# Two convolutions in 32x32 products: blocks of two adjacent rows, or of the two halves of one image

## The chip, the cores and the metric

The kernel runs on one core of a Trainium2 chip. The time is the device time of one execution in microseconds; the median of several runs is compared. The five engines that appear below are TensorE (PE, with its weight loads as PEld), VectorE (DVE), ScalarE (ACT), GpSimd (POOL) and SyncE (SP, which here only issues transfers).

## The reference

Four layers of the form x = x + conv(groupnorm(x)) act on a tensor of 16 images, 16 channels and 256 x 256 pixels in float32. Only the first two layers matter here:

```python
x = x + _L0_conv_ref(_gn(x), L0_conv_weight)      # 3x3 convolution, circular in y and x (written with FFTs)
x = x + _L1_conv_ref(_gn(x), L1_conv_filter_w)    # 5x5 kernel filter_w[..., :, None] * eye(5), zero padding of 2
```

The group norm has 8 groups of 2 channels, over a whole image. The second kernel is diagonal: it takes the pixel (y + d, x + d) for d from -2 to 2, so it has five taps, each with a 16 x 16 matrix over channels. Layers 2 and 3 (a pole-residue layer and a quantised 3x3 convolution) follow; they read the result of layer 1 from DRAM.

## The kernel before

Layers 0 and 1 form one stage, with an instruction order that is written out by hand. Each image b is held in SBUF as `xs[b % 2]`, its layer-1 input as `vs[b % 2]`. The 128 partitions are four quads of 32 (`quads`), and each quad holds 16 channels times two adjacent rows of the image, the parity of the row being the upper or lower 16 lanes (`lanes(p, i)`). The four quads of x are four bands of rows.

A matmul works on one quad of the input and one quad of the output, so it is a 32x32 product, and sixteen such tiles of the array can work at once. With two adjacent rows in the block, 16 input lanes and 16 output lanes of different parity stand for different offsets in y. For layer 0, the outputs of the lower lanes are also shifted by one column, so that 2 row steps times 4 column steps, eight products of 512 columns (two row pairs), cover the 3x3 taps (`products0`, L449). For layer 1 three products of 257 columns (one row pair) cover the five diagonal taps (`products1`, L471). The residual is added by putting ones into the scaled weights (`scaled`).

`load` (L269 to L274) brings an image in four parts, each as DMAs of 16 partitions and 8 or 9 rows, 1 KB per row, on SP's queue. `edges` (L374, L375) copies the circular columns on POOL, `see` (L378) takes statistics on DVE. The `Chain` class makes the group norm: aggregate, a product with the `group` table on PE (L311), another (L322), a reciprocal root on DVE, and a constant per lane (L340); POOL scales the weights (L389).

`leave0` (L455, L456) takes a bank out of PSUM on ACT into `vs` and DVE takes its statistics. `halo` (L433) copies the rows that neighbouring bands need, on POOL for one side and on ACT for the other. `pads` (L417 to L422) fills the padding with the mean on POOL. `leave1` (L479 to L489) takes layer 1's bank out on ACT, mends the outer column on DVE, takes statistics and stores x2d in DMAs of 16 partitions, half of them issued from POOL and half from SP. PSUM has seven banks for these products (`ps_v`) and one for the group norm.

The order of all this comes from `at(time, function, ...)`: every step gets a time in columns of a product, and the steps are issued on their engines sorted by it. `WEAVE` is the period of one image; layer 1 of image b is woven into layer 0 of image b + 1:

```python
    WEAVE = 4 * 8 * 2 * N + 8 * 3 * (N + 1)          # 22,552 columns
...
        t0 = b * WEAVE + (0, 4096, 9734, 16143)[u] + 1024 * p                                        # unit0
...
        t0 = (b + 1) * WEAVE + (8192, 8963, 13830, 14601, 15372, 20239, 21010, 21781)[s] + 1024 * q  # unit1
```

The index p (or q) is the quad that is contracted, the row group of the array. In these times each row group always has one unit in work, and the four are 1,024 columns apart. Within a step the four products go to the four output quads.

Of the kernel before, what the change touches and what calls it, by code (L numbers as in the profile page):

```python
# [71 lines left out]
def constants():  # L72
# [10 lines left out]
    def sin(a, b):  # L83
# [38 lines left out]
        "group": (p % 16 // 2 == q % 16 // 2) / 16.0,  # L122
        "first": p == 2 * c8,
# [13 lines left out]
        "res": np.concatenate([1.0 * (p % 32 == np.arange(32)[None, :] + 16),  # L137
                               1.0 * (p % 32 + 16 == np.arange(32)[None, :])], 1),
# [29 lines left out]
def layers(ctx, tc, x, w0, w1, w3, sw, bias, ty, tx, p1a, p1b, p1c, p2a, p2b, p2c, resa, resb,  # L168
# [61 lines left out]
    PW = N + 3  # L230
    VW = N + 5
    XS = N // 8 + 1
    WEAVE = 4 * 8 * 2 * N + 8 * 3 * (N + 1)

    def by_rows(d, p, i, lo, n):

        return d.rearrange("c (k t) w -> c t k w", t=2)[:, i, 32 * p + lo : 32 * p + lo + n, :]

    def lanes(p, i):
        return slice(32 * p + 16 * i, 32 * p + 16 * i + 16)  # L240

    quads = [slice(32 * r, 32 * r + 32) for r in range(4)]

    with ExitStack() as es:
# [10 lines left out]

        xs = [wp.tile([P, XS, PW], F32, tag=f"x{k}", name=f"x{k}") for k in range(2)]
        vs = [wp.tile([P, 4, 10, VW], F32, tag=f"v{k}", name=f"v{k}") for k in range(2)]

        def load(b, part):

            lo, n = 8 * part, 8 if part < 3 else 9
            for p in (0, 2, 1, 3):
                for i in range(2):
                    to, rows_ = xs[b % 2][lanes(p, i)], x[b]
                    k0, n_, at = lo, n, lo
                    if i == 0:
                        k0 -= 1
                        if p == 0 and part == 0:
                            nc.sync.dma_start(to[:, 0, 1 : 1 + N], rows_[:, N - 1, :])  # L269
                            k0, n_, at = 0, n - 1, 1  # L270
                    elif p == 3 and part == 3:
                        nc.sync.dma_start(to[:, XS - 1, 1 : 1 + N], rows_[:, 0, :])
                        n_ = n - 1
                    nc.sync.dma_start(to[:, at : at + n_, 1 : 1 + N], by_rows(rows_, p, 1 - i, k0, n_))  # L274

        for part in range(4):
            load(0, part)
        group, first, ones = table(wp, "group"), table(wp, "first"), table(wp, "ones")
        even, odd = table(wp, "real"), table(wp, "imag")
        res, eye = table(wp, "res"), table(wp, "eye")  # L280
        wt0 = wp.tile([P, 8, 32], F32, tag="wt0", name="wt0")
        nc.sync.dma_start(wt0.rearrange("p n m -> p (n m)"), w0)
        wt1 = wp.tile([P, 3, 32], F32, tag="wt1", name="wt1")
# [6 lines left out]
        for k, (w, n) in enumerate(((wt0, 8), (wt1, 3))):  # L290
            red = cell(32, "red")
            V.tensor_reduce(red, w.rearrange("p n m -> p m n"), AX.X, ADD)
            whole = wp.tile([P, 4, 32], F32, tag=f"sum{k}", name=f"sum{k}")
            V.tensor_scalar(whole, bc(red, 1, 4), -0.25, None, MUL)
            sums.append(whole.rearrange("p q m -> p (q m)"))
# [75 lines left out]
        def edges(b, part):  # L371
            lo, n = 8 * part, 8 if part < 3 else 9
            s = xs[b % 2][:, lo : lo + n]
            Q.tensor_copy(s[:, :, 0:1], s[:, :, N : N + 1])  # L374
            Q.tensor_copy(s[:, :, 1 + N : 3 + N], s[:, :, 1:3])  # L375

        def see(b, k):
            V.bn_stats(stats_of(st0s, b, "st0")[:, k, :], xs[b % 2][:, 2 * k : 2 * k + 2, 1 : 1 + N])  # L378
# [7 lines left out]
        def scaled(b, kind):  # L386
            n, wt, eyes = ((8, wt0, ((1, 0), (6, 1))), (3, wt1, ((1, None),)))[kind]
            w = sp.tile([P, n, 32], F32, tag=f"w{kind}s", name=f"w{kind}s")
            Q.tensor_scalar(w, wt, chains[b, kind].rs[:, 0:1], None, MUL)  # L389
            for k, e in eyes:  # L390
                tt(Q, w[:, k], w[:, k], eye if e is None else res[:, 32 * e : 32 * e + 32], ADD)
            (w0s, w1s)[kind][b] = w
# [17 lines left out]
        def pads(b):  # L410

            v, mu = vs[b % 2], chains[b, 1].g3[:, 0:1, 0]
            flat = v.rearrange("p g n w -> p (g n) w")
            me, mo = cell(1, "me"), cell(1, "mo")
            tt(Q, me, mu, even, MUL)
            tt(Q, mo, mu, odd, MUL)
            Q.tensor_copy(v[quads[0], 0, 0, :], mu[quads[0]].to_broadcast([32, VW]))  # L417
            Q.tensor_copy(v[quads[3], 3, 9, :], mu[quads[3]].to_broadcast([32, VW]))
            for lo in (0, VW - 2):
                Q.tensor_copy(flat[:, :, lo : lo + 2], bc(bc(mu[:, 0], 1, 40), 2, 2))  # L420
            Q.tensor_scalar(flat[:, :, 2:3], flat[:, :, 2 + N : 3 + N], odd, me, MUL, ADD)
            Q.tensor_scalar(flat[:, :, 2 + N : 3 + N], flat[:, :, 2 + N : 3 + N], even, mo, MUL, ADD)  # L422

        def halo(b, q, side):

            v, eng = vs[b % 2], (Q.tensor_copy if side else nc.scalar.copy)
            frm = (q + (1 if side else -1)) % 4
            g_to, g_from = slice(0, 4), slice(0, 4)
            if side and q == 3:
                g_to, g_from = slice(0, 3), slice(1, 4)  # L430
            if not side and q == 0:
                g_to, g_from = slice(1, 4), slice(0, 3)
            eng(v[quads[q], g_to, 9 if side else 0, 3 : 3 + N], v[quads[frm], g_from, 1 if side else 8, 3 : 3 + N])  # L433

        def unit0(b, u, p):

            t0 = b * WEAVE + (0, 4096, 9734, 16143)[u] + 1024 * p
            for n in range(8):
                at(t0 + 512 * n, products0, b, u, p, n)
            at(t0 + 4095.5, leave0, b, u, p)  # L440

        def products0(b, u, p, n):
            if n == 0:
                open_[p] = ps_v.tile([P, 512], F32, tag="ps_v", name="ps_0")
            ps = open_[p]
            e, t = divmod(n, 4)
            for q in range(4):
                lo = 8 * q + 2 * u + e
                nc.tensor.matmul(ps[quads[q]].rearrange("p (k w) -> p k w", k=2), lhsT=w0s[b][quads[p], n, :],  # L449
                                 rhs=xs[b % 2][quads[p], lo : lo + 2, t : t + N], start=n == 0, stop=n == 7)  # L450

        def leave0(b, u, p):
            ps = open_[p]
            to = vs[b % 2][:, p, 1 + 2 * u : 3 + 2 * u, 3 : 3 + N]
            nc.scalar.activation(to, ps.rearrange("p (k w) -> p k w", k=2), AF.Identity, bias=c0s[b])  # L455
            V.bn_stats(stats_of(st1s, b, "st1")[:, 4 * p + u, :], to)  # L456

        def unit1(b, s, q):

            t0 = (b + 1) * WEAVE + (8192, 8963, 13830, 14601, 15372, 20239, 21010, 21781)[s] + 1024 * q  # L460
            for n in range(3):
                at(t0 + 257 * n, products1, b, s, q, n)
            at(t0 + 770.5, leave1, b, s, q)

        def products1(b, s, q, n):
            if n == 0:
                open_[q] = ps_v.tile([P, 512], F32, tag="ps_v", name="ps_1")
            ps = open_[q]
            for p in range(4):
                lo = 2 * n  # L470
                nc.tensor.matmul(ps[quads[p], 0 : N + 1], lhsT=w1s[b][quads[q], n, :],  # L471
                                 rhs=vs[b % 2][quads[q], p, s + n, lo : lo + N + 1], start=n == 0, stop=n == 2)

        def leave1(b, s, q):
            ps, h = open_[q], s // 4
            if s % 4 == 0:
                outs[q] = op.tile([P, 4, N + 1], F32, tag="x2s", name="x2s")
            o = outs[q]
            nc.scalar.activation(o[:, s % 4, :], ps[:, 0 : N + 1], AF.Identity, bias=c1s[b])  # L479
            if s % 4 < 3:  # L480
                return
            e = cell(4, "fix")
            V.tensor_scalar(e, o[:, :, 0], odd, None, MUL)
            V.scalar_tensor_tensor(o[:, :, N], o[:, :, N], even, e, MUL, ADD)
            for k in range(2):
                V.bn_stats(stats_of(st2s, b, "st2")[:, 4 * q + 2 * h + k, :], o[:, 2 * k : 2 * k + 2, 1 : 1 + N])
            for i in range(2):
                for p in (0, 2, 1, 3):
                    (nc.sync if i else Q).dma_start(by_rows(x2d[b], p, i, 8 * q + 4 * h, 4),  # L489
                                                    o[lanes(p, i), :, 1 - i : 1 - i + N])  # L490

        for b in range(B):
            t = b * WEAVE
            for p in range(4):
                for u in range(4):
                    unit0(b, u, p)
                for s in range(8):
                    unit1(b, s, p)
            for q in range(4):
                at(t + 7800 + 700 * q, halo, b, q, 1)  # L500
                at(t + 23400 + 250 * q, halo, b, q, 0)
            for k in range(4):
                if b:
                    at(t - WEAVE + 900 + k if b > 1 else -30000 + k, load, b, k)
                at(t - WEAVE + 6500 + 3300 * k, edges, b, k)
                for n in range(4):
                    at(t - WEAVE + 6500 + 3300 * k + 300 * n, see, b, 4 * k + n)
# [926 lines left out]
```

## Time and profile before

| what | value |
|---|---|
| median of three runs | 4160.77 us (4160.36 to 4162.11) |
| the profiled execution | 4147.03 us |
| its span, first to last instruction | 4145.2 us |
| granted TensorE clock, mean | 0.943 |
| PE, PEld, DVE, ACT, POOL busy | 85, 67, 67, 53, 46% of the span |
| one slice of the page (a fortieth) | 103.6 us |

The page gives busy time for each engine and for groups of instructions: line, engine, operation, tiles, shape, count, then busy microseconds and mean nanoseconds of one, then the idle time before them and what ended it. In the view of one line's instructions, three durations are the smallest, median and largest in nanoseconds, and the two times after them are the first and last start. In the timeline, merged instructions stand with start, length and count. In the windows, each engine has its busy time and count, in the order PE, PEld, DVE, ACT, POOL (only PE and PEld where one line is asked for), then the granted clock, the DMA share and GB/s. A record that overlaps a window is counted as busy in it.

### The profile page before, as it was taken

What the parts mean: (1) busy time and instruction counts of PE and PEld (TensorE: products, weight loads), DVE (VectorE), ACT (ScalarE), POOL (GpSimd) and SP (SyncE); (2) the same over time, 40 slices, a digit from 0 to 9 for tenths busy, and PEclk for the clock granted to TensorE, in tenths of its full rate; (3) what the DMA queues carried; (4) which work ended last, traced back from release to release, by engine and by line L of the source; (5) the groups of instructions that cost most, each with busy time, mean ns of one, the idle gap of its engine ahead of it and who ended that gap; (6) DMA issues with size and microseconds to landing.
All of it is one profiled execution on the core that took longest, in us unless ns stands there. A gap on an engine that the chain in (4) does not pass through costs nothing. (4 is left out here: it accounts for less than half of the span.)

```text
span 4145.2 us, 175747 instructions
## 1 busy us (share of the span) xinstructions
PE 3539.6 (85%) x77336; PEld 2766.3 (67%) x77336; DVE 2759.2 (67%) x5153; ACT 2189.7 (53%) x3985; POOL 1906.9 (46%) x2878
## 2 busy tenths in 40 slices
PE   4899988989968999999966777776999999996777
PEld 3555555555537999999955555555888888883444
DVE  3555555555548888887765656654677777668998
ACT  1344444444425444444466666665454544448998
POOL 0334343433333434443276666663666766662222
PEclk9899999999959999999999999998999999997898
DMA  7666576756343545455356666667888888868998
GB/s 91 104 128 135 120 137 117 133 120 130 84 116 128 189 152 168 150 185 174 130 164 189 186 184 186 187 185 196 224 232 237 237 231 246 248 185 313 337 353 304
DMA packets 510974, 758.03 MB, mean 183 GB/s; under 512 B 53697, under 2 KB 419137, under 8 KB 501953
## 3 DMA queue, kind: packets, MB, share of 16 engines
q1 hardware_dynamic: 467200, 612.26, 54.2%
q0 software_dynamic: 43008, 134.52, 10.6%
q8 instruction: 608, 9.96, 1.0%
q14 instruction: 158, 1.29, 0.1%
HBM read 410.52 MB, written 336.07 MB: 180 GB/s over the span
## 5 line engine op out<-in xcount | busy, mean ns | idle before, releaser
L449 PE MATMUL ps<-x,w0s 32*32 32x512 f32 x16384 | 936.5, 643 | 36.1 <-issue 35.9
L471 PE MATMUL ps<-v,w1s 32*32 32x257 f32 x12288 | 649.6, 409 | 14.1 <-issue 12.3
L489 POOL DMA_DIRECT2D x2d<-x2s x512 | 261.9, 518 | 502.9 <-ACT x2s L479 375.4
L771 ACT ACTIVATE y<-ps_y,bc 128x384 f32<-128x384 f32 x512 | 296.3, 581 | 350.9 <-PE ps_y L769 350.5
L449 PEld LDWEIGHTS ps<-x,w0s 32*32 32x32 f32 x16384 | 344.6, 106 | 199.5 <-issue 144.3
L988 PE MATMUL ps_m<-z,sk 128*32 128x64 f32 x16384 | 333.7, 225 | 166.9 <-issue 127.3
L471 PEld LDWEIGHTS ps<-v,w1s 32*32 32x32 f32 x12288 | 349.2, 108 | 178.7 <-issue 112.5
L193 POOL TENSOR_TENSOR w<-rq 128x512 f32<-128x512 f32 x256 | 335.1, 1330 | 260.4 <-ACT rq L1131 259.7
L988 PEld LDWEIGHTS ps_m<-z,sk 128*32 128x32 f32 x16384 | 301.3, 113 | 220.4 <-issue 149.6
L479 ACT ACTIVATE x2s<-ps,c 128x257 f32<-128x257 f32 x512 | 237.8, 476 | 396.3 <-PE ps L471 307.9
L456 DVE BATCH_NORM_STATS2 st<-v 128x6 f32<-128x512 f32 x256 | 177.0, 692 | 371.5 <-ACT v L455 371.0
L1130 PE MATMUL ps_o<-exp,fs 128*128 128x128 f32 x2048 | 400.5, 278 | 10.9 <-ACT fs L1178 10.8
L1129 PE MATMUL ps_o<-c_last,zt 128*128 128x128 f32 x2048 | 399.1, 277 | 0.0
L1275 PE MATMUL ps_c<-q,wt 64*64 64x512 bf16 (+1 forms) x4608 | 295.3, 408 | 100.4 <-ACT o L1322 83.4
L193 DVE TENSOR_TENSOR ob<-ps_m,other 128x256 f32<-128x256 f32 x512 | 193.3, 419 | 276.4 <-ACT other L1014 262.5
L909 PE MATMUL ps_s<-t,l 128*32 128x258 f32 x4096 | 322.4, 396 | 51.7 <-issue 33.0
L1129 PEld LDWEIGHTS ps_o<-c_last,zt 128*128 128x128 f32 x2048 | 324.2, 194 | 61.3 <-issue 61.3
L193 POOL TENSOR_TENSOR u<-xt 128x512 f32<-128x512 f32 x128 | 167.3, 1308 | 392.6 <-DVE qd L193 279.8
L1275 PEld LDWEIGHTS <-wt 64*64 64x64 bf16 x4800 | 182.2, 115 | 213.7 <-issue 147.0
L1130 PEld LDWEIGHTS ps_o<-exp,fs 128*128 128x128 f32 x2048 | 314.3, 194 | 12.8 <-ACT fs L1178 12.8
L766 PE MATMUL ps_y<-c_y,qd 128*128 128x128 f32 x2048 | 322.2, 280 | 0.3
L769 PE MATMUL ps_y<-hat,qd 128*128 128x128 f32 x2048 | 314.4, 276 | 0.0
(238 smaller groups left out, 7723.0 us busy)
## 6 DMA issues: line engine op xcount, KB each, us to landing
xt<-x2d SPq DMA_DIRECT2D x256, 512.0 KB, 4.3
z<-alphad SPq DMA_DIRECT2D x258, 258.0 KB, 4.1
mixd<-ob SPq DMA_DIRECT2D x256, 256.0 KB, 4.8
ot<-mixd SPq DMA_DIRECT2D x256, 256.0 KB, 6.2
x3d<-xt SPq DMA_DIRECT2D x128, 512.0 KB, 5.3
xt<-x3d SPq DMA_DIRECT2D x64, 1024.0 KB, 9.0
out_dram<-xt POOLq DMA_DIRECT2D x64, 1024.0 KB, 9.1
x<-in_x_dram SPq DMA_DIRECT2D x384, 128.0 KB, 6.0
```

What stands on the lines that cost most here:

```text
L193: eng.tensor_tensor(o, a, b, op)
L449: nc.tensor.matmul(ps[quads[q]].rearrange("p (k w) -> p k w", k=2), lhsT=w0s[b][quads[p], n, :], rhs=xs[b % 2][quads[p], lo : lo + 2, t : ...
L471: nc.tensor.matmul(ps[quads[p], 0 : N + 1], lhsT=w1s[b][quads[q], n, :], rhs=vs[b % 2][quads[q], p, s + n, lo : lo + N + 1], start=n == 0, ...
L489: (nc.sync if i else Q).dma_start(by_rows(x2d[b], p, i, 8 * q + 4 * h, 4), o[lanes(p, i), :, 1 - i : 1 - i + N])
L766: nc.tensor.matmul(to[:, :, a, :], lhsT=v[:, c, a, i % 2, :], start=a == 0, stop=a == 1, rhs=y1[:, a].rearrange("p (r f) -> p r f", r=2))
L769: nc.tensor.matmul(ps[:, 2 * P : 3 * P], lhsT=v[:, c, a, i % 2, :], start=False, stop=a == 1, rhs=hats[0][:, a, i], skip_group_check=True)
L771: nc.scalar.activation(y[:, c, :], ps[:, 0 : 3 * P], AF.Copy, scale=bc2[:, b, i // 2, 0:1])
L909: nc.tensor.matmul(ps[at : at + 32, d, 0 : 2 * NX], lhsT=ls[h][:, k + d - k0, n], rhs=t2[:, h, k + d].rearrange("p r x -> p (r x)"), start ...
L988: nc.tensor.matmul(to, lhsT=sk[:, x_], rhs=z[:, :, x_], start=True, stop=True)
L1129: nc.tensor.matmul(ps[:, a, c, :], lhsT=zts[d][:, a, c, :], rhs=last[:, c, :], start=True, stop=False)
L1130: nc.tensor.matmul(ps[:, a, c, :], lhsT=fs[:, d, a, :], rhs=ey[:, d, c, :], start=False, stop=True)
L1275: nc.tensor.matmul(o, lhsT=wt[half[h], w, :], rhs=src, start=i == 0, stop=i == len(work[0]) - 1)
```

## The change

A block of 32 lanes now holds 16 channels times the two halves of the image: lane 2c + h is channel c, rows 128h to 128h + 127. Both halves use the same taps, so a block's weights are the same 16 x 16 matrix twice, and layer 0 takes nine products of 512 columns, layer 1 five products of 512 columns (two rows). The period becomes 29,272 columns.

In x, the rows of a block of ten lie one behind another with no space between them, and a tap that moves by one column reads across the row's end. The outer two columns of layer 0 come out wrong by that; `leave0` leaves them out, and `sides` makes them with nine taps of products of 16 columns (8 rows, 2 columns). Statistics of the first unit of each band are taken after `sides`. The wrapped copies of columns (`edges`) are gone. `load` brings 32 partitions at a time with ten rows that are contiguous in DRAM and in SBUF, the overlap of neighbouring blocks included, and the edges of the image by small DMAs. The halo rows of `vs` are moved by four DMAs on SP (`below`, `above`) instead of copies on POOL and ACT. `leave1` loses the mending of the outer column; its stores are of 32 partitions and 4 KB each, all issued from POOL. The steps of the group norm stand at other times. The host code that lays out the weights, and the tables `group`, `first`, `upper` and `lower`, follow the new lanes.

```diff
-    PW = N + 3
-    VW = N + 5
-    XS = N // 8 + 1
-    WEAVE = 4 * 8 * 2 * N + 8 * 3 * (N + 1)
...
+    XR = 10 * N
+    MARGIN = 16
+    VR, VW = 36, N + 4
+    UNIT0, UNIT1 = 9 * 2 * N, 5 * 2 * N
+    AT0 = (0, 5208, 12376, 22104)
+    AT1 = (9816, 16984, 19544, 26712)
+    WEAVE = 29272
...
+        def by_rows(d):
+            return d.rearrange("c (h q p r) w -> q p (c h) r w", h=2, q=4, p=4)
...
+        def load(b, q):
+            to, frm = xs[b % 2][:, q], by_rows(x[b])
+            whole = x[b].rearrange("c (h y) w -> (c h) y w", h=2)
+            lo, hi = (0 if q else 1), (10 if q < 3 else 9)
             for p in (0, 2, 1, 3):
...
+                y = 32 * q + 8 * p - 1
+                nc.sync.dma_start(to[quads[p], lo:hi, :], whole[:, y + lo : y + hi, :])
+            if q in (0, 3):
+                edge = 0 if q == 0 else 9
+                for p in range(4):
+                    y = 32 * q + 8 * p - 1 + edge
+                    if 0 <= y < 128:
+                        nc.sync.dma_start(to[quads[p], edge, :], whole[:, y, :])
+                    else:
+                        for h in range(2):
+                            nc.sync.dma_start(to[32 * p + h : 32 * p + 32 : 2, edge, :],
+                                              x[b][:, (128 * h + y) % N, :])
...
-        def halo(b, q, side):
-
-            v, eng = vs[b % 2], (Q.tensor_copy if side else nc.scalar.copy)
...
+        def below(b):
+            v = vs[b % 2][:, :, 2 : 2 + N]
+            nc.sync.dma_start(v[0:96, VR - 2 :, :], v[32:128, 2:4, :])
+            nc.sync.dma_start(v[96:128:2, VR - 2 :, :], v[1:32:2, 2:4, :])
+
+        def above(b):
+            v = vs[b % 2][:, :, 2 : 2 + N]
+            nc.sync.dma_start(v[32:128, 0:2, :], v[0:96, VR - 4 : VR - 2, :])
+            nc.sync.dma_start(v[1:32:2, 0:2, :], v[96:128:2, VR - 4 : VR - 2, :])
...
+        def sides(b, p):
+            ps = ps_v.tile([P, 512], F32, tag="ps_v", name="ps_e")
+            for n, (dy, dx) in enumerate(taps):
+                for q in range(4):
+                    src = xs[b % 2][quads[p], q, 1 + dy : 9 + dy, :]
+                    src = (src[:, :, 254:256], src[:, :, ::-255], src[:, :, 0:2])[1 + dx]
+                    nc.tensor.matmul(ps[quads[q], 0:16].rearrange("p (r w) -> p r w", w=2), lhsT=w0s[b][quads[p], n, :],
+                                     rhs=src, start=n == 0, stop=n == 8)
+            to = vs[b % 2][:, 2 + 8 * p : 10 + 8 * p, 2 : 2 + N][:, :, ::-255]
+            nc.scalar.activation(to, ps[:, 0:16].rearrange("p (r w) -> p r w", w=2), AF.Identity, bias=c0s[b])
+            taken(b, 0, p)
...
-                nc.tensor.matmul(ps[quads[q]].rearrange("p (k w) -> p k w", k=2), lhsT=w0s[b][quads[p], n, :],
-                                 rhs=xs[b % 2][quads[p], lo : lo + 2, t : t + N], start=n == 0, stop=n == 7)
+                lo = MARGIN + XR * q + N * (1 + dy + 2 * u) + dx
+                nc.tensor.matmul(open_[p][quads[q]], lhsT=w0s[b][quads[p], n, :], rhs=flat[b % 2][quads[p], lo : lo + 512],
+                                 start=n == 0, stop=n == 8)
...
-                nc.tensor.matmul(ps[quads[p], 0 : N + 1], lhsT=w1s[b][quads[q], n, :],
-                                 rhs=vs[b % 2][quads[q], p, s + n, lo : lo + N + 1], start=n == 0, stop=n == 2)
+                r = 8 * p + 2 * u + n
+                nc.tensor.matmul(open_[q][quads[p]].rearrange("p (k w) -> p k w", k=2), lhsT=w1s[b][quads[q], n, :],
+                                 rhs=vs[b % 2][quads[q], r : r + 2, n : n + N], start=n == 0, stop=n == 4)
...
-            V.tensor_scalar(e, o[:, :, 0], odd, None, MUL)
-            V.scalar_tensor_tensor(o[:, :, N], o[:, :, N], even, e, MUL, ADD)
...
-                    (nc.sync if i else Q).dma_start(by_rows(x2d[b], p, i, 8 * q + 4 * h, 4),
-                                                    o[lanes(p, i), :, 1 - i : 1 - i + N])
...
+                    to = by_rows(x2d[b])[q, p, :, 2 * u - 2 : 2 * u + 2, :].rearrange("c r w -> c (r w)")
+                    Q.dma_start(to, outs[q][quads[p]])
...
+                at(s + 4700, sides, b, p)
...
+            at(t + 4700 + 3600, below, b)
+            at(t + AT0[3] + UNIT0 + 3100, above, b)
...
-            for kind, t0 in ((0, t - WEAVE + 17800), (1, t + WEAVE + 1500)):
+            for kind, t0 in ((0, t - WEAVE + 19500), (1, t + WEAVE + 1300)):
```

## The prediction

> **What bounds the kernel now.** I read the page's slices first, then the groups, the life of the two product lines, and last the timeline and windows inside one batch.
>
> ```profile
> PE   4899988989968999999966777776999999996777
> PEclk9899999999959999999999999998999999997898
> L449 PE MATMUL ps<-x,w0s 32*32 32x512 f32 x16384 | 936.5, 643 | 36.1 <-issue 35.9
> L471 PE MATMUL ps<-v,w1s 32*32 32x257 f32 x12288 | 649.6, 409 | 14.1 <-issue 12.3
> L471 PE MATMUL ps<-v,w1s x12288: 372/377/632, 137.5 to 1199.0; 32*32 32x257 f32 x199
> L449 PE MATMUL ps<-x,w0s x16384: 584/609/1059, 57.5 to 1140.7; 32*32 32x512 f32 x200
> ```
>
> One slice is 103.6 us, so the first eleven and a half hold layers 0 and 1, and PE stands at eight or nine tenths there. The count says that every product of the source is two records (16 batches x 512 products of layer 0 make 8,192; the trace has 16,384). Layer 0 runs from 57.5 to 1140.7 us: 67.7 us a batch; the last batch's layer 1 ends at 1199. The rest of the kernel reads x2d, whose layout the change leaves alone, so everything is decided in these 1,199 us.
>
> Busy PE says little, because up to sixteen 32x32 products run at once. What one product takes from the stream is in the timeline and in short windows (layer 0's row ahead of layer 1's for the same stretch):
>
> ```profile
> 604.03 3.62 PE L449 MATMUL ps<-x,w0s 32*32 32x512 f32 x98 [0.79 <-issue]
> 607.58 0.38 PE L340 MATMUL ps_c<-rm,sum 128*128 128x1 f32 x2
> 607.90 1.13 PE L449 MATMUL ps<-x,w0s 32*32 32x512 f32 x28
> 611.07 6.06 PE L449 MATMUL ps<-x,w0s 32*32 32x512 f32 x128 [2.04 <-issue]
> 568.00:570.00 2.00, 1.84 (x31) 0.43 (x24) 1.00 0.34 61
> 568.00:570.00 2.00, 2.00 (x72) 1.47 (x66) 1.00 0.34 61
> 598.00:616.00 18.00, 15.17 (x379) 7.95 (x361) 8.60 (x24) 4.93 (x9) 7.48 (x21) 0.91 1.11 191
> 692.00:732.00 40.00, 37.67 (x1215) 23.35 (x1209) 24.65 (x56) 17.84 (x37) 11.06 (x26) 1.00 0.49 93
> ```
>
> 98 records of 512 columns in 3.62 us, less the last one's own 0.59, are 31 ns each. In 568 to 570 us, 24 starts of 512 columns (24 x 31 = 0.74 us) leave 1.26 us for 66 starts of 257 columns: 19 ns each. These are the good prices. A batch has 1,024 records of the one and 768 of the other: 31.7 + 14.6 = 46.3 us. It takes 67.7, so 21.4 us are lost.
>
> Where? I went through the starts of all PE records from 137 to 1142 us (14.8 batches). Gaps over 0.4 us sum to 12.5 us a batch: 5.4 ahead of the group-norm products (PE waits for DVE's `mv`), 5.5 where a 16 KB packet of the instruction queue had ended 1.1 to 1.9 us before the next start, 1.5 other. The fetch gaps are seen above: runs of 128 records (with their weight loads, 256 instructions) parted by 0.79 and 2.04 us, at a DMA share of 1.11, while x is loaded. In 692 to 732, with no load, 1,209 weight loads pass in 40 us; in 598 to 616, 361 in 18. The remaining 8.9 us are thin stretches: 46.3 becomes 55.2, a factor of 1.19 (bank handovers, colder clock).
>
> DVE (24.65 of 40 us), ACT (17.84) and POOL (11.06) have room: PE's stream bounds this stage.
>
> **The change, part by part.** *Layer 0's products*: 9 taps instead of 8, so 1,152 records x 31 ns = 35.7 us a batch, +4.0. *Layer 1's*: 5 taps over 512 columns (4 units) instead of 3 over 257 (8 units): 640 records x 31 = 19.8 us against 14.6, +5.2. *Small products of the outer columns*: 4 x 36 a batch, 288 records of 16 columns, in four bursts on one row group. No such record is in the trace. From below: 32 records of L988 (64 columns, 32-column weights) pass in 0.73 us, less 0.23 for the last: 16 ns, 4.6 us a batch. From above: in one tile 18 such steps follow each other, and if each waits for its weight load (104 ns, L449's median) a burst takes 1.9 us, a batch 7.5. They can't be a gain, being added work. I take 18 ns, 5.2 us, near L988's row, since the loads there overlap. The Trainium skill (TensorEngine Tiling (Array Packing), section Instruction Overhead) speaks against such products: one column costs as much as sixty, about 60 cycles; at 25 ns my estimate from that page is 7.2 us, and the sum 2 us a batch higher. The trace's 16 ns for 64 columns is under that, so the row stands.
>
> Good prices after: 35.7 + 19.8 + 5.2 = 60.7 us, against 46.3.
>
> *What multiplies it*: today 1.19. Layer 1 takes a new bank 32 times a batch now and 16 after, plus 4 for the sides; with seven banks, fewer handovers mean fewer thin stretches. Between 1.0 and 1.19 I take the middle, 1.095: 66.5 us.
>
> *Stalls*: the layer-0 chain begins 2,800 columns after its last statistics are due instead of 500, and the weights are due 6,172 columns ahead of use instead of 1,752, so of the 5.4 us of group-norm gaps I take 1.5 off. Fetches rise with instructions (2,080 against 1,792 records, x1.16). Loads fall from 1 KB runs into 16 partitions to 10 KB runs into 32, but 5.24 MB a batch instead of 4.33. One thing raises the 5.5 us, another lowers it: I leave them. The Trainium skill (Runtime: NRT & Kernel Launch, section Instruction fetch mechanics) has 16 KiB refills mostly hidden; by that rule the 5.5 us would be absent before and after. The gaps of 0.79 and 2.04 us at exact runs of 128 contradict it. Stalls: 11 us.
>
> A batch: 66.5 + 11 = 77.5 us, +9.8; fifteen batches carry both layers: +147 us.
>
> *Start*: first product at 57.5 us; DVE waits until 41.58 for `wt`, which lies behind 36 loads of x at 124 GB/s. After, 5.24 MB: at 124 GB/s 42 us against 35 (+7); if twice the partitions double the rate, 21 (-14). I take -8. *Tail*: 768 records of layer 1 take the 41 us from 1158 to 1199 at a clock of 0.50. By records 640 would take 34 us (-7), by columns (640 x 512 against 768 x 257) 68 (+27); by the good prices 19.8 / 14.6 gives 56: +15.
>
> *Off the path, at nothing*: DVE loses `fix` and L484 (29 us each), ACT and POOL the halo copies L433 (63.6 and 62.6 us), POOL the edge copies. ACT writes 16 x 0.685 us for layer 1 instead of 32 x 0.476 and four small ones (0.2 us, the 128x1 form, to 0.48). The 1,024 stores of 64 KB become 512 of 128 KB, all on POOL, which issues 512 today at 0.52 us. POOL waits there for ACT's `x2s`; queued behind are the scaled weights and `pads`, with 6,172 columns (at 2.65 ns, 16 us) and 4,616 (12 us) in hand; if late, the first products wait and each us counts whole. SP gains four halo transfers a batch. `above` waits for layer 0's last leave, with the next loads behind it, which must wait for the same products' reads anyway; it has 9,276 columns (25 us) until layer 1, against 3 to 9 us for a landing. `below` queues behind the loads and is needed 18,400 columns later.
>
> Sum: 147 - 8 + 15 = +154 us on the profiled 4147.03 (span 4145.2 and 1.8 around it): 4301. The median of the runs, 4160.77, stands 13.7 above the profiled one: **4315 us**.
>
> **Rivals.** *Short products are no cheaper today* (0.14). All of the 55.2 us less 31.7 for layer 0, over 768, is 30.6 ns for 257 columns, as much as for 512; 692 to 732 speaks for it (1,209 loads in 40 us, 33 ns each, half of them short). Then 512 columns come free and only the added records cost: 60.7 + 11 = 71.7, +4.0 x 15 = 60, less 8: 4213. Against it is the 19 ns of 568 to 570.
>
> *Nothing gets denser* (0.14). The factor stays 1.19 because clock and imbalance make it, not banks, and stalls grow with fetches: 72.2 + 12.5 x 1.16 = 86.7, +19 x 15 = 285, with +7 and +15: 4468. For it: the clock's cold slices, and bursts that leave three row groups unfed.
>
> *Loads stop starving the fetch: faster* (0.07). Long runs into 32 partitions end the saturated stretches (1.11 at 598 to 616). If the 5.5 us vanish, group norm shrinks to 4 and the factor to 1.0: 60.1 + 4 = 64.1, -3.6 x 15 - 14 = -68: 4093. It decides once all loss on top of 60.7 is under 7.0 us a batch; today it is 21.4, so two thirds must go.
>
> No change within 0.2% (8 us, about what can be told from no change here) needs the pieces to cancel: 0.02.
>
> **How the numbers follow.** The forecast, slower by 60 to 250, has 0.63; with both slower rivals 0.91 for slower, 0.07 faster, 0.02 same. The range 4215 to 4465 holds the forecast and reaches both slower rivals' own times, about half of each; left out are the other halves, the faster case and the null, some 0.2.
>
> **What the profile would show.** 18,432 records for layer 0 and 10,240 for layer 1, both 32x512, 4,608 of 16 columns; layer 0 ending near 1,290 us; dense runs still at 31 ns. Wrong if layer 0's batches take under 70 us: then look for runs of 128 without gaps during loads, or for short products that always cost 31 ns. Wrong upwards if bursts of the sides last over 2 us or POOL's queue holds back `w0s` or `pads`.

## The result, and the profile after

The changed kernel takes 4332.92 us (median of 4 runs, 4327.85 to 4340.07), against 4161.44 for the kernel before: a ratio of 1.0413, 95% interval 1.0395 to 1.0431, 171 us more. The profiled execution took 4332.12 us, its span is 4330.4. The spans of the two profiles lie 185 us apart, 14 more than the medians, because the profiled execution of the kernel before was 14 us under its median.

From the page after, the slices of PE and of its clock and the group of layer 0:

```profile
PE   5989999899997899999996777776899999996776
PEclk9889989889997999999999999998899999998999
L458 PE MATMUL ps<-x,w0s 32*32 32x512 f32 x18432 | 1040.7, 667 | 36.9 <-issue 36.4
```

From the views of the two lines, with first and last start, and from the groups of the first 1,400 us, the small products:

```profile
L473 PE MATMUL ps<-v,w1s x10240: 584/587/1058, 156.4 to 1374.8; 32*32 32x512 f32 x197
L458 PE MATMUL ps<-x,w0s x18432: 584/609/1058, 46.9 to 1319.6; 32*32 32x512 f32 x199
L446 PE MATMUL ps_e<-x,w0s 32*32 32x16 f32 x4608 | 102.6, 200 | 57.1 <-issue 57.0
```

The records are those forecast: 18,432, 10,240 and 4,608. Against the profile before, the stage divides like this. The first product of layer 0 starts at 46.9 us instead of 57.5: -10.6. From there to the last one, 1272.8 us instead of 1083.2, 79.5 a batch instead of 67.7: +189.6. From there to layer 1's last, 55.2 instead of 58.3: -3.1. What follows the stage takes 2955.6 instead of 2946.2: +9.4, in code that the change left alone. The sum is the 185.2 us between the two spans.

Inside a batch, one place stands out. The timeline of PE at the first burst of small products of image 7, while the next image is loaded:

```profile
617.17 0.65 PE L446 MATMUL ps_e<-x,w0s 32*32 32x16 f32 x33
620.64 0.45 PE L446 MATMUL ps_e<-x,w0s 32*32 32x16 f32 x19 [2.83 <-issue]
620.89 1.06 PE L458 MATMUL ps<-x,w0s 32*32 32x512 f32 x2
```

33 small products pass in 0.65 us, then PE has nothing for 2.83 us and waits for no semaphore, and the long product after that takes 1.06 us instead of 0.59: the clock has halved. The windows (PE, PEld, DVE, ACT, POOL, clock, DMA share, GB/s) show three stretches of the same kernel: the four bursts of image 7 beside a load, the woven products after them, and the four bursts of the last image, beside which nothing is loaded:

```profile
616.00:641.00 25.00, 20.04 (x572) 10.97 (x559) 7.50 (x13) 3.92 (x8) 4.11 (x10) 0.66 0.76 224
641.00:660.00 19.00, 19.00 (x603) 15.46 (x602) 11.35 (x19) 6.67 (x10) 0.00 (x0) 1.00 0.02 4
1263.00:1277.00 14.00, 12.48 (x555) 8.06 (x532) 2.84 (x6) 3.92 (x8) 3.16 (x8) 1.00 0.15 44
```

559 weight loads take 25 us at a clock of 0.66 in the first, 532 take 14 at full clock in the last. In the middle one, 602 records of 512 columns pass at 31.6 ns each. So the thinnest stretch of a batch is the one where small products meet a load. How much of the 171 us it explains is for the runs to show.

### The profile page after: what moved, and what is told of

The parts are those of the page before. It is cut to its first block, busy times and chain, and to the rows that moved or that the text cites. A ratio compares the mean times of both kernels' runs of the same rounds, so it can differ in the third digit from the quotient of the medians.

```text
span 4330.4 us, 182523 instructions
## 1 busy us (share of the span) xinstructions
PE 3726.7 (86%) x81944; PEld 2904.7 (67%) x81944; DVE 2705.6 (62%) x4897; ACT 2087.0 (48%) x3729; POOL 1809.8 (42%) x2646
## 5 line engine op out<-in xcount | busy, mean ns | idle before, releaser
L458 PE MATMUL ps<-x,w0s 32*32 32x512 f32 x18432 | 1040.7, 667 | 36.9 <-issue 36.4
L473 PE MATMUL ps<-v,w1s 32*32 32x512 f32 x10240 | 675.7, 606 | 0.8 <-POOL v L420 0.8
L485 POOL DMA_DIRECT2D x2d<-x2s x512 | 251.8, 498 | 918.6 <-ACT x2s L480 828.8
L458 PEld LDWEIGHTS ps<-x,w0s 32*32 32x32 f32 x18432 | 386.2, 108 | 219.6 <-issue 179.3
L473 PEld LDWEIGHTS ps<-v,w1s 32*32 32x32 f32 x10240 | 361.3, 104 | 151.2 <-issue 66.4
L464 ACT ACTIVATE v<-ps,c 128x508 f32<-128x508 f32 x256 | 176.2, 688 | 464.5 <-PE ps L458 464.5
L1128 PEld LDWEIGHTS ps_o<-exp,fs 128*128 128x128 f32 x2048 | 313.8, 194 | 11.3 <-ACT fs L1176 11.3
```

The lines of the kernel that those rows point to most:

```text
L458: nc.tensor.matmul(open_[p][quads[q]], lhsT=w0s[b][quads[p], n, :], rhs=flat[b % 2][quads[p], lo : lo + 512], start=n == 0, stop=n == 8)
L473: nc.tensor.matmul(open_[q][quads[p]].rearrange("p (k w) -> p k w", k=2), lhsT=w1s[b][quads[q], n, :], rhs=vs[b % 2][quads[q], r : r + 2, ...
L485: Q.dma_start(to, outs[q][quads[p]])
L1128: nc.tensor.matmul(ps[:, a, c, :], lhsT=fs[:, d, a, :], rhs=ey[:, d, c, :], start=False, stop=True)
```

## The experiments

Two theories were open after that, P and S; F and R were added after the first runs. **P**, the prediction's prices by columns (31 ns for 512, 19 for 257, 18 for a small product); **S**, the bursts of small products cost far more than their time, by idle PE and clock; **F**, PE runs short of instructions beside loads; **R**, a batch costs its records, whatever their columns.

Ratios are to the kernel before on the same chip, which varied from chip to chip (medians of 4147 to 4167 us); a ratio is turned into time with 4161 us, so the changed kernel stands at +172 (164 to 179).

**One tap.** The small products keep one tap of nine, the middle one:

```diff
-            for n, (dy, dx) in enumerate(taps):
+            for n, (dy, dx) in ((4, taps[4]),):
...
-                                     rhs=src, start=n == 0, stop=n == 8)
+                                     rhs=src, start=True, stop=True)
```

> The changed kernel with one tap of nine in the small products (the outer two columns of layer 0 lack the other eight taps). Theory P, the prediction's prices: 256 of 288 records a batch go at 18 ns, 4.6 us a batch, 16 batches: -74 us, 4259 us. Theory S, from the profile after: the bursts run out of instructions, leave three row groups unfed and are followed by a half clock, so the small products cost 12 to 15 us a batch: -190 to -240 us, 4095 to 4145 us, and layer 0's half-clock slices of 10 to 20 us in every batch are gone.

Measured: 4211.23 us, ratio 1.0115 (1.0063 to 1.0166), +48. The 256 records are worth 124 us, with the two intervals put together 101 to 147: 7.7 us a batch, 30 ns a record. P's 74 us is outside; so are the 190 to 240 of S. From the first to the last small product of an image the mean of images 2 to 13 falls from 23.1 us to 10.3, and the clock between 137 and 1185 us is 0.964 (0.899 in the changed kernel, 156 to 1320 us). About a third of the 12.8 us that leave this stretch comes back elsewhere in the batch, which shrinks by 8.4 in the trace. So the 30 ns are what a record costs in its place, with the stalls and the clock that go with it.

**Taps spread out.** The same products, 128 columns apart in the order instead of in a burst:

```diff
...
-                at(s + 4700, sides, b, p)
+                for n in range(9):
+                    at(s + 4700 + 128 * n, sides, b, p, n)
```

> The changed kernel with the nine taps of the small products set 128 columns apart instead of in one burst; the work is the same. Theory P: no difference (within 10 us of 4333). Theory S: between two taps other row groups are fed and instructions are used at half the pace, so the bursts of 2 to 6 us and the half clock behind them mostly go: -80 to -160 us, 4170 to 4250 us.

Measured: 4333.23 us, ratio 1.0402 (1.0357 to 1.0447): no difference. That it is the burst, as an order of products, is refuted. The stretch becomes 25.9 us long, and the clock there is no better (0.65 against 0.66).

**Loads behind the small products:**

```diff
-                    at(t - WEAVE + 800 + q if b > 1 else -50000 + q, load, b, q)
+                    at(t - WEAVE + 9000 + 1800 * q if b > 1 else -50000 + q, load, b, q)
...
-                    at(t - WEAVE + 5000 + 3500 * q + 400 * n, see, b, q, n)
+                    at(t - WEAVE + 12400 + 1800 * q + 400 * n, see, b, q, n)
```

> The changed kernel with the loads of the next image issued at 9000 to 14400 columns, behind the small products, instead of at 800; statistics follow later. If the loads starve the instruction fetch in the bursts (theory S, first form): bursts shrink to the 1.5 to 2.3 us of the last image, which has no loads beside it, -50 to -100 us. If the bursts alone bring the clock down (theory S, second form), or by theory P: within 20 us of 4333; fetch gaps then move to where the loads are.

Measured: 4322.51 us, ratio 1.0371 (1.0323 to 1.0419); 17 us less, within the intervals. Yet the stretch of the small products shrank from 23.1 to 15.5 us. What it gave was lost again where the loads now are: instructions were fetched slowly there, for other products (gaps behind a late packet still take 7.7 us a batch, 7.8 in the changed kernel). The form of S that put the cost on the fetch beside loads in the bursts alone had 50 to 100 us, which is not borne out.

**No loads, in both kernels.** The loads of images 2 to 15 are dropped (the kernel before in the same way):

```diff
-                if b:
-                    at(t - WEAVE + 800 + q if b > 1 else -50000 + q, load, b, q)
+                if b == 1:
+                    at(-50000 + q, load, b, q)
```

> The changed kernel without the loads of images 2 to 15 (the first two images are used again). Theory F, from the intervals between instruction fetches in the run after: 4.2 us with little DMA traffic, 6.5 to 7.8 us at a DMA share over 0.8, in 41 of 181: some 9 us a batch are lost to loads, -125 us, about 4210 us, and the bursts of small products take 1.5 to 2.3 us. If loads are not what starves the fetch: within 20 us of 4333.

> The kernel before without the loads of images 2 to 15. Theory F: 48 fetches at a DMA share over 1.0 fall from 5.9 to 4.2 us, 6 us a batch, -85 us, about 4075 us. The distance to the changed kernel without loads is then the price of the products alone: by the prediction's good prices 14.4 us a batch (230 us), by records (2,080 against 1,792 at 31 ns) 8.9 us (143 us).

Measured: the changed kernel 4173.74 us, ratio 1.0046 (1.0026 to 1.0066), 153 us less than with loads; the kernel before 4050.83, ratio 0.9761 (0.9726 to 0.9795), 99 us less. F stands: loads cost both kernels their time on PE, and the changed one some 54 us more. In the table further down most of it is gaps: 9.6 of the changed kernel's 10.2 us a batch, 5.1 of the other's 6.5. The four bursts of an image now look like those of the last one, here image 8 (its small products run from 614.1 to 625.8 us):

```profile
614.00:627.00 13.00, 11.63 (x534) 6.88 (x529) 5.14 (x10) 3.90 (x8) 2.61 (x8) 1.00 0.12 34
```

529 records in 13 us at full clock, against 559 in 25. Without loads the two kernels are 123 us apart. By records it was to be 143, by columns 230. So most of the 171 us remains without any load beside the small products.

**Paced loads.** Each of the sixteen large DMAs of an image is issued by itself, 900 columns apart:

```diff
...
-                if b:
-                    at(t - WEAVE + 800 + q if b > 1 else -50000 + q, load, b, q)
+                if b == 1:
+                    at(-50000 + q, load, b, q)
+                for j in range(4 if b > 1 else 0):
+                    at(t - WEAVE + 800 + 3600 * q + 900 * j, load_one, b, q, j)
...
-                    at(t - WEAVE + 5000 + 3500 * q + 400 * n, see, b, q, n)
+                    at(t - WEAVE + 6600 + 3600 * q + 300 * n, see, b, q, n)
```

> The changed kernel with the sixteen large DMAs of a load issued 900 columns (some 2.4 us) apart instead of all at once, so that few wait in the DMA engines at a time; the same bytes. Theory F in the form that an instruction fetch waits behind queued packets: fetch intervals over 6 us go, -40 to -90 us, 4245 to 4295 us. In the form that any load beside the fetch slows it: no difference or a loss, as with the spread loads of the kernel before (+1.2%).

**Spread loads in the kernel before:**

```diff
-                    at(t - WEAVE + 900 + k if b > 1 else -30000 + k, load, b, k)
+                    at(t - WEAVE + 900 + 3300 * k if b > 1 else -30000 + k, load, b, k)
```

> The kernel before with the four parts of each load 3300 columns apart instead of all at 900. If the saturated DMA engines (share 1.05 to 1.16) cause the fetch gaps of 5.5 us a batch, most of them go: -45 to -80 us, 4080 to 4115 us, and runs of 128 products without a gap in the profile. If not: within 10 us of 4161.

Measured: paced, 4331.25 us, ratio 1.0429 (1.0396 to 1.0461), no difference; spread, 4208.71 us, ratio 1.0116 (1.0068 to 1.0164), slower by 48 us. Neither edit took the loads off the DMA engines as meant. SP issues an image's loads over some 26 us instead of 25 in the paced kernel, over 34 instead of 25 in the spread one. Of the slices of 1 us between 200 and 1100 us, 26% have a DMA share over 1.0 instead of 24%, and 38% instead of 33%. Fetch intervals over 6 us stay at 34 of some 180 with pacing. So these runs do not tell whether a fetch merely stands behind too many queued packets. They show that longer contact with loads was worse for the kernel before: its gaps behind a late packet grew from 5.5 to 7.7 us a batch. What a fetch waits for is left open.

The fetches themselves can be counted. Each 16 KB packet of the instruction queue carries 256 instructions of PE, 128 records with their weight loads (608 packets in the kernel before, for 154,672 instructions of PE). The times from one packet to the next, between 200 and 1100 us (median, with the count):

| DMA share meanwhile | before | changed | changed, no loads | half both |
|---|---|---|---|---|
| under 0.2 | 3.92 us (47) | 4.20 (97) | 4.01 (136) | 3.77 (100) |
| 0.8 to 1.0 | 4.14 (15) | 6.45 (24) | 4.97 (13) | 6.31 (19) |
| over 1.0 | 5.81 (48) | 7.79 (17) | none | 7.18 (25) |

The longer intervals are not the clock's alone: over those 48 of the kernel before its mean was 0.96.

**Half the columns in layer 1.** Taps 1 to 4 take one row of the two, so the second row lacks them:

```diff
-                r = 8 * p + 2 * u + n
+                r, k = 8 * p + 2 * u + n, 2 if n == 0 else 1
...
-                                 rhs=vs[b % 2][quads[q], r : r + 2, n : n + N], start=n == 0, stop=n == 4)
+                                 rhs=vs[b % 2][quads[q], r : r + k, n : n + N], start=n == 0, stop=n == 4)
```

> The changed kernel with taps 1 to 4 of layer 1 over one row (256 columns) instead of two; as many products and instructions, half the columns in 512 records a batch (the second row of each pair lacks four taps). Theory P, PE pays for columns (31 against 19 ns): 6.1 us a batch, -98 us, 4235 us. Rival, PE pays for each record whatever its length: no difference beyond 20 us.

Measured: 4310.03 us, ratio 1.0379 (1.0346 to 1.0412): 14 us less, give or take 16. P's 98 is refuted for these 512 records a batch; R's "no difference beyond 20" holds.

**Half the columns in both layers**, the same in `products0`:

```diff
+                lo, w = MARGIN + XR * q + N * (1 + dy + 2 * u) + dx, 512 if n == 0 else 256
...
-                                 start=n == 0, stop=n == 8)
+                nc.tensor.matmul(open_[p][quads[q], 0:w], lhsT=w0s[b][quads[p], n, :], rhs=flat[b % 2][quads[p], lo : lo + w],
+                                 start=n == 0, stop=n == 8)
```

> The changed kernel with all taps but the first of both layers over half the columns (half of each unit lacks the other taps); all 2,080 records a batch stay. Theory R, a batch costs its instructions (256 in 3.3 to 4.2 us without loads, more beside loads) and not its columns: within 40 us of 4333. Theory P, columns: 1,536 records a batch at 19 instead of 31 ns, 18 us a batch, -295 us.

Measured: 4207.12 us, ratio 1.0144 (1.0092 to 1.0195): 112 us less, give or take 23. Neither theory: 1,536 records lost 256 columns each and 4.6 ns each, where P had 12 and R had none. The mean clock of the stage fell too, to 0.82 (140 to 1223 us) from 0.90, so a loss to the clock could hide a gain from the columns. Where the DMA share is under 0.2 there is no such loss: the interval between packets is 3.68 us where the clock was under 0.6 (18 intervals) and 3.77 where it was over 0.95 (72). Beside loads it can't be told apart.

**Outer columns in a quarter of the products.** One product covers all four bands (64 columns) and goes to one quad; four ACT instructions bring it to its places:

```diff
+            got = ps[quads[p], 0:64].rearrange("p (q r w) -> p q r w", q=4, w=2)
             for n, (dy, dx) in enumerate(taps):
-                for q in range(4):
-                    src = xs[b % 2][quads[p], q, 1 + dy : 9 + dy, :]
...
+                src = xs[b % 2][quads[p], :, 1 + dy : 9 + dy, :]
...
+                nc.tensor.matmul(got, lhsT=w0s[b][quads[p], n, :], rhs=src, start=n == 0, stop=n == 8)
...
+            for q in range(4):
+                nc.scalar.activation(to[quads[q]], got[:, q], AF.Identity, bias=c0s[b][quads[p]])
```

> The changed kernel with the outer columns of all four bands in one product: 36 products of 64 columns a batch instead of 144 of 16, the same sums, taken out by four ACT instructions instead of one. Theory R: 216 records fewer at the 33 ns that one tap showed, 7.1 us a batch, -114 us, ratio to the kernel before about 1.014. Theory P (18 ns): -62 us, ratio 1.026.

Measured: 4224.28 us, ratio 1.0175 (1.0127 to 1.0222): 99 us less, give or take 21. That is as many small columns in a quarter of the instructions. R's 114 holds, P's 62 doesn't.

**Two rows in the kernel before.** If records count, the kernel before has 768 of only 257 columns. Here its layer 1 takes two rows by 256 columns at a time, and the one column that this leaves out comes from 48 products of 8 columns a batch:

```diff
...
+                    nc.tensor.matmul(ps[quads[p], 0:8], lhsT=w1s[b][quads[q], n, :],
+                                     rhs=vs[b % 2][quads[q], p, n : n + 8, 2 * n], start=n == 0, stop=n == 2)
...
-                lo = 2 * n
-                nc.tensor.matmul(ps[quads[p], 0 : N + 1], lhsT=w1s[b][quads[q], n, :],
-                                 rhs=vs[b % 2][quads[q], p, s + n, lo : lo + N + 1], start=n == 0, stop=n == 2)
+                lo = 2 * n + 1
+                nc.tensor.matmul(open_[q][quads[p]].rearrange("p (k w) -> p k w", k=2), lhsT=w1s[b][quads[q], n, :],
+                                 rhs=vs[b % 2][quads[q], p, 2 * u + n : 2 * u + n + 2, lo : lo + N],
+                                 start=n == 0, stop=n == 2)
...
```

> The kernel before with layer 1 in products of two rows by 256 columns (12 a unit of 512 columns, half as many as now) and the outer column of the odd rows by 48 products of 8 columns a batch: 1,504 records a batch instead of 1,792, with about as many columns. Theory R: 288 records at 31 to 33 ns, 9 us a batch, about -145 us, 4005 to 4030 us, faster than both kernels. Theory P: long products cost 31 against 19 ns, 384 x 31 + 96 x 18 = 13.6 us against 14.6: -15 us.

Measured: 4189.66 us, ratio 1.0103 (1.0063 to 1.0143), slower by 43 us: a miss of R as it was stated. The waits show where half of it went: those of the kernel before (100 to 1140 us), of this one (100 to 1180 us) and then of the next one (100 to 1060 us), which takes it up. Gaps grew by 7.4 us a batch, 3.6 of them ahead of group-norm products (9.1 in all, 4.3 in the next kernel):

```profile
PEld ps_gn L311 <- DVE mv L306: 62.9, 29, 3.4
PE ps_gn L311 <- DVE mv L306: 39.8, 28, 2.5
```

```profile
PEld ps_gn L311 <- DVE mv L306: 104.8, 29, 5.0
PE ps_gn L311 <- DVE mv L306: 78.5, 28, 4.1
```

```profile
PEld ps_gn L311 <- DVE mv L306: 22.3, 16, 1.8
PE ps_gn L311 <- DVE mv L306: 7.6, 13, 0.9
```

**The same, with its order rewritten.** With two rows PE reaches the group norm longer before DVE has its statistics, and everything behind the waiting product waits too. Layer 0's last units and the chain get other times, here against the kernel with two rows; layer 1's units, the loads, the statistics and the halo copies move as well:

```diff
...
-            t0 = b * WEAVE + (0, 4096, 9734, 16908)[u] + 1024 * p
+            t0 = b * WEAVE + (0, 4096, 8192, 15366)[u] + 1024 * p
...
-            for kind, t0 in ((0, t - WEAVE + 17800), (1, t + WEAVE + 2265)):
+            for kind, t0 in ((0, t - WEAVE + 16200), (1, t + WEAVE + 700)):
-                at(t0 + 500, step, b, kind, "means")
+                at(t0 + 1200, step, b, kind, "means")
...
```

> The kernel with layer 1 in products of two rows and 1,504 records a batch, with its order rewritten: layer 0's last unit ends 1,524 columns earlier, and the group-norm products stand 1,000 to 1,200 columns behind the start of their chain instead of 500. In the two-row kernel before it, gaps took 19.9 us of a batch of 69.9 (9.1 of them ahead of group-norm products, 5.5 in the kernel before) and the rest 50.1 us, against 55.2. If the late chain ate what the fewer records gave: gaps of 10 to 13 us, a batch of 60 to 63 us, -75 to -120 us against the kernel before, ratio 0.97 to 0.98, faster than both. If fewer records give nothing because the time is set elsewhere (DVE's statistics, the loads): gaps grow again and the ratio stays at 1.00 to 1.01.

Measured: 4011.7 us, ratio 0.9657 (0.963 to 0.9684): 143 us faster than the kernel before, and faster than both. What two rows and the new times gave each is not shown, since the kernel before was not run with the new times alone. By the table below, what remains outside the gaps fell by 6.6 us a batch against the kernel before, the gaps by 1.7. In its groups the whole of layers 0 and 1 is 22,528 long records and 1,536 small ones:

```profile
L449 PE MATMUL ps<-x,w0s 32*32 32x512 f32 x16384 | 820.2, 614 | 66.0 <-issue 65.5
L483 PE MATMUL ps<-v,w1s 32*32 32x512 f32 x6144 | 441.7, 626 | 0.0
L473 PE MATMUL ps_e<-v,w1s 32*32 32x8 f32 x1536 | 38.6, 177 | 2.8 <-issue 1.7 <-POOL v L420 0.8 <-POOL v L421 0.3
```

**All kernels side by side.** From the traces: time of a batch (layer 0's first to last start over 16), gaps over 0.4 us between the starts of PE records, what remains, and that per record:

| kernel | batch us | gaps us | records | mean columns | rest, ns a record |
|---|---|---|---|---|---|
| before | 67.7 | 12.5 | 1,792 | 403 | 30.8 |
| changed | 79.5 | 15.9 | 2,080 | 443 | 30.6 |
| changed, one tap | 71.1 | 10.2 | 1,824 | 503 | 33.4 |
| changed, outer columns in a quarter | 73.0 | 9.5 | 1,864 | 495 | 34.1 |
| changed, layer 1 halved | 79.0 | 15.2 | 2,080 | 380 | 30.7 |
| changed, both halved | 73.5 | 17.2 | 2,080 | 254 | 27.1 |
| before, no loads | 61.2 | 7.4 | 1,792 | 403 | 30.0 |
| changed, no loads | 69.3 | 6.3 | 2,080 | 443 | 30.3 |
| two rows | 69.9 | 19.9 | 1,504 | 480 | 33.3 |
| two rows, order rewritten | 59.4 | 10.8 | 1,504 | 480 | 32.3 |

Between a mean of 254 and 495 columns what remains goes from 27 to 34 ns a record, so half the columns save about a fifth of it. Where small products were left out, most of the gain is not in what remains but in the gaps: they shrink by 5.7 us a batch with one tap and by 6.4 with the outer columns in a quarter, while what remains goes from 63.6 us to 60.9 and 63.5. This fits F: a small record is quick in itself, but it uses up instructions, and PE then waits for more.

## Why the prediction was right, and where its steps were not

The forecast of 4315 us is 18 below the measured 4333, and the direction and place (PE's stream in layers 0 and 1) are right. But the sum holds partly because wrong terms cancel. Outside the gaps it had +11.3 us a batch, where +8.4 were measured; for the gaps -1.5, where +3.4 were measured. Between the two traces it had 154 us against 185; by medians the miss is smaller because the profiled execution before lay 14 us under its median, and that is luck.

- *Layer 1's longer products, +5.2 us a batch.* Wrong. Taking away 256 columns from 512 records a batch returned 14 us in all, 0.9 a batch, where its prices say 6.1. The step that failed is the price of 19 ns for 257 columns: it came from 2 us with 90 starts, a rate that no fetch interval carries on (128 records take 3.9 us there at the median at a DMA share under 0.2, 31 ns each, and never less than 3.3 us). With two rows the time outside the gaps fell by 5.2 and 6.6 us a batch, where these prices give 1.0. The first rival, short products no cheaper, was right on this.
- *Small products, 5.2 us a batch at 18 ns.* Mis-sized. 256 of 288 cost 7.7 us a batch, 30 ns each. The row of L988 gave their time while instructions last; the upper bound from weight loads (7.5 us) was aimed at the wrong mechanism. The remark that bursts would leave row groups unfed stood with the second rival, at 0.14; the runs show idle PE and a halved clock, but spreading the taps out did not help, so it is not their order, while a quarter of the instructions for the same columns did help. Its own sign of being wrong upwards did appear: 38 of the 48 bursts of images 2 to 13 last over 2 us, 3.3 at the mean (1.9 without loads).
- *Layer 0's ninth tap, +4.0 us.* Not tested by itself. With layer 1's change, long records come out even (1,792 before and after). The kernel with one tap, which has 32 small ones besides, is 48 us over the kernel before.
- *The factor of 1.095 and stalls of 11 us.* The time outside gaps is 63.6 us a batch, 1.05 times the good prices; gaps are 15.9. Group-norm gaps fell from 5.4 to 3.0 us, more than the 1.5 us off that were forecast. Gaps that fit a late fetch rose from 5.5 to 7.8; the forecast left them. The others rose from 1.5 to 5.3, 1.8 of them beside small products.
- *Start, -8.* Measured -10.6. DVE's wait for `wt` ends at 30.7 instead of 41.6 us, though more bytes lie ahead: the DMA engines moved 5.38 MB in the first 28 us, against 4.50 in the first 40 before.
- *Tail, +15.* Measured -3.1. The term by good prices failed here as well; by records it was -7. The clock differed, 0.72 against 0.57 before, so the tail does not settle the price of a record.
- *Cover.* POOL's stores, `w0s`, `pads` and the halo transfers held almost nothing up: PE waits 0.4 us for `w0s` and 0.8 for the edges of `v` in the whole stage.
- *Third rival.* Its 60.1 us should be the 60.7 of the good prices; that shifts its time by 9 us and no conclusion.

Of the two rules weighed: the Trainium skill (TensorEngine Tiling (Array Packing), section Instruction Overhead) gives each product an overhead of about 60 cycles. While instructions last, 33 small ones, on several tiles at once, passed in 0.65 us less the last one's 0.2, 14 ns each, under the 25 that the prediction estimated from it. Yet in the sum they cost 30, with the gaps.

The other one, instruction refills that are mostly hidden (Runtime: NRT & Kernel Launch, section Instruction fetch mechanics), differs from the table of fetches: 5.8 to 7.8 us a block at a DMA share over 1.0, and 2 to 3 us of idle PE at a time.

Open: what a fetch waits for beside a load (neither pacing nor spreading lowered the DMA share), why the clock halves just there, what the ninth tap costs by itself, and the 9.4 us behind the stage.

## What to carry to other kernels

Where products are small and many, count the instructions of the TensorE queue before the columns, and price a record from a stretch that is longer than one 256-instruction block. Short products for an edge can cost nearly as much each as full ones (30 ns here); put several edges into one product, or make the main products longer. When PE gets shorter, move the steps that it waits for as well: two rows gave nothing until the order around the group norm was rewritten, and then 143 us.

## What the runs showed of the hardware

The shortest interval between two 16 KB instruction packets of PE lay between 3.2 and 3.5 us in every kernel, whatever the products, and the later stages have none under 3.2 either: 256 instructions in 3.3 us are 26 ns for a product with its weight load, though 33 in a row can start 14 ns apart. Halving the columns of 1,536 of 2,080 records moved the median at a DMA share under 0.2 only from 4.20 to 3.77 us, and there half the clock did not lengthen it (3.68 against 3.77). This fits a limit of the fetch itself; no run here tested that alone.

At a DMA share over 1.0 the same block takes 6 to 8 us at the median. The share alone does not decide: between 0.8 and 1.0 a block took 4.14 us in the kernel before and 6.45 in the changed one.
